# A graph-network layer on one core: row broadcasts in eight transfers, loads held back by the planner, three `g` banks and two `a` banks, 11 gather buffers

## The chip, the cores and the metric

One core of a Trainium2 chip runs the whole program. The time is device microseconds of one execution, from the first to the last work of the core; lower is better. The kernel before took 502.47 us (median of three runs, 501.62 to 507.94).

## The reference

Node features `x` (6,250 x 128, f32) and 100,000 edges, sorted by destination, each with a source, a destination and a type 0 or 1. For every edge a message is made from the source's row, with one of two weight matrices by type; messages are added up per destination; the node's own product is added; then relu, the residual and a layer norm:

```
Xs = X[src]
m_data = Xs @ W_data.T + b_data
m_ctrl = Xs @ W_control.T + b_control
msg = jnp.where((edge_types == 0)[:, None], m_data, m_ctrl)
agg = jax.ops.segment_sum(msg, dst, num_segments=X.shape[0])
out = relu(agg + (X @ W_self.T + b_self))
x   = layernorm(x + out)
```

## The kernel before

**The message table.** A message depends only on the source and the type, so the kernel makes all 2 x 6,250 of them once. 25 steps of two node blocks each (L467 to L501) load pieces of `xt` (the transposed features), multiply in f32 on TensorE (L483), and split each result into three bf16 parts, 3 x 128 = 384 columns: ACT writes the first part (L488), TensorE subtracts it (L491), ACT or VectorE writes the second (L494), VectorE the third (L495). `m3` holds the 98 tiles (49 node blocks x 2 types) of 128 rows in SBUF; a copy goes to DRAM as `table` (L499).

**Windows.** The first 27 x 160 destinations are done window by window, in groups of 1, 2, 4, 4, 4, 4, 4 and 4 windows (`GROUPS`). `ranks` (L611) prepares a group: it loads the edges of each window (`win`), makes one-hots of their source tiles (`hots`, L681), counts with matmuls into the bank `rk` (for the first group `ga`) which place each edge takes among the edges of its tile (L692, read by VectorE at L706), and scatters source row and destination of the edge to that place with matmuls into `vt` (L742; 21 for each window). The result is copied to `vs` (L755), stored to DRAM as `packed` (L762) and read back. Edges beyond 32 places of a tile go into a list of 64, whose messages are gathered from `table` by GpSimd (`sr`, L851) and moved to `gl` (L858).

`sums` (L884) then works through the windows. One transfer of 784 KB broadcasts the window's 32 x 98 row numbers to all 128 partitions (`rows`, L893); VectorE compares them with the partition number, in two halves (L901), which makes the one-hots of the sources; VectorE makes the one-hots of the destinations, `hot2` (L909). Then come 25 steps `g` of four tiles each. **Stage 1** (L922): four matmuls, one for each strip of 32 output partitions, pick 4 x 32 messages out of `m3` into a PSUM bank `g`. **The copy** (L425): ACT, rarely VectorE, turns the bank into bf16, `gs`. **Stage 2** (L936, L939): four matmuls of 384 and three of 128 columns add the 128 messages to the window's 160 destinations, in the PSUM bank `a`. After the last step VectorE adds up the three parts (L551) and ACT copies the rest (`bs`, L949); `close` (L514) does relu, residual, layer norm and the stores.

**Gathered destinations.** The other 1,930 destinations lie in 16 blocks of up to 125. GpSimd gathers 128 messages at a time from `table` (`t_msg`, L1016, 263 times, eight buffers), VectorE makes one-hots for six gathers at once (`t_hot`, L1010, two buffers), and TensorE adds them up in the bank `ga` (L1023). This runs beside the windows and fills in between their matmuls.

**Order.** Every instruction goes through `Plan` (L92). At build time it lays all of them on a time axis, with a duration, a due time and assumed latencies (`HOP`, `lat`) for each, takes on each engine the ready operation with the earliest due time, and writes the resulting order out. On the chip each engine keeps that order: what waits holds up all that stands behind it on its engine. SyncE (SP) starts nearly all transfers. Transfers started by SP and ACT use eight completion semaphores in turn, and a start waits until the transfer eight places before it has landed. PSUM has eight banks: four `g`, one `a`, and one each for `rk`, `ga` and `vt`. The product steps of the start use the `g` and `a` banks (L470).

Of the kernel before, what the change touches and what calls it, by code (L numbers as in the profile page):

```python
# [10 lines left out]
F32 = mybir.dt.float32  # L11
BF16 = mybir.dt.bfloat16
I32 = mybir.dt.int32
# [8 lines left out]
P = 128  # L22
# [60 lines left out]
class Op:  # L83
    __slots__ = ("alts", "due", "lat", "deps", "after", "left", "ready", "start", "end", "out",
                 "index", "engine")

    def __init__(self, alts, due, lat):
        self.alts, self.due, self.lat = alts, due, lat
        self.deps, self.after, self.out = [], [], []


class Plan:  # L92
    HOP = {"PE": 0.22, "ACT": 0.15, "DVE": 0.11, "POOL": 0.12, "SP": 0.12}
    OWN = {"DVE": 0.09, "ACT": 0.12}
    OTHER = 0.5

    def __init__(self):
        self.ops, self.rings = [], {}

    def add(self, engine, dur, fn, due, r=(), w=(), lat=0.0):  # L100
        alts = engine if isinstance(engine, list) else [(engine, dur, fn)]
        op = Op(alts, due, lat)
        op.index = len(self.ops)
        self.ops.append(op)
        deps = set()
        for items, writes in ((r, False), (w, True)):
            for item in items:
                b, key = item if isinstance(item, tuple) else (item, None)
                for k, (ws, rs) in b.keys.items():
                    if key is None or k is None or k == key:  # L110
                        deps.update(ws)
                        if writes:
# [12 lines left out]
        return op  # L125
# [4 lines left out]
    def run(self):  # L130
# [31 lines left out]
        while len(order) < n:  # L162
# [20 lines left out]
            for o in op.out:  # L183
                if op in o.deps:
                    same = op.lat == 0 and all(a == e for a, _, _ in o.alts)
                    lag = self.OWN.get(e, 0.0) if same else op.lat + self.HOP[e]
                    o.ready = max(o.ready, op.end + lag)
                    o.left -= 1
                if op in o.after:
                    o.ready = max(o.ready, op.start)  # L190
                    o.left -= 1
                if not o.left:
                    offer(o)
                    o.left = -1
# [47 lines left out]
def sums_over_windows(ctx, tc, x, xt, edges, w, bias, out, total):  # L242
# [16 lines left out]
    def C(shape, dtype, name):  # L259
        return Buf(plan, const, shape, dtype, name, 1)  # L260

    T0 = 36.0
    TW = 13.0
    LAT = 0.2
    G0, G1 = 0.0, -4
    GC = 1.3
    SPD = 0.45


# [4 lines left out]
    w_sb = C([D, D3], F32, "w_sb")  # L274
    b1 = C([1, D3], F32, "b1")
    add("ACT", 0.1, lambda: A.dma_start(w_sb.t, w), 0.0, [], [w_sb], lat=2.5)
    add("ACT", 0.1, lambda: A.dma_start(b1.t, bias), 0.0, [], [b1], lat=2.5)

# [83 lines left out]
    def count_rows():  # L362
# [8 lines left out]
    vec(0.5, 1, lambda: V.tensor_copy(row_i.t, row_f.t), [row_f], [row_i])  # L371
    er = C([NBD, RL, 3], I32, "er")
    add("POOL", 1.0, lambda: G.indirect_dma_start(
        out=er.t.rearrange("p k c -> p (k c)"), out_offset=None,
        in_=edges.rearrange("(p k) c -> p (k c)", k=RL),
        in_offset=bass.IndirectOffsetOnAxis(ap=row_i.t[:, 0:1], axis=0)),
        0.5, [row_i], [er], lat=3.5)
# [3 lines left out]
    vec(0.6, RL, lambda: V.tensor_copy(dst_f.t, er.t[:, :, 1]), [er], [dst_f])  # L381
    vec(0.6, RL, lambda: V.tensor_scalar(less.t, dst_f.t, bound_p.t, None, op0=ALU.is_lt,
# [15 lines left out]
    def load_edges(b, n, out_, due, buf, key, engine):  # L398
# [13 lines left out]

    left = C([1, D3], F32, "left")
# [3 lines left out]
    add("ACT", 0.4, lambda: A.copy(brows.t[:1], b1.t), 0.5, [b1], [brows])  # L417
    vec(0.5, D3, lambda: V.tensor_sub(left.t, b1.t, brows.t[:1]), [b1, brows], [left])
    add("ACT", 0.4, lambda: A.copy(mid.t, left.t), 0.5, [left], [mid])
    vec(0.5, D3, lambda: V.tensor_sub(brows.t[2 * R : 2 * R + 1], left.t, mid.t), [left, mid],  # L420
        [(brows, 2)])
# [19 lines left out]
    XB = [12, 12, 12, 13]  # L441
    XC = 4 * WN
    xts = []
# [167 lines left out]
    def ranks(gi, w0, nw, when, step, engines):  # L611
# [237 lines left out]
        for pr in range(nh):  # L849
# [34 lines left out]
    def sums(gi, w0, nw, placed):  # L884
# [5 lines left out]
        for i in range(nw):  # L890
            due = T0 + (w0 + i) * TW
            sp = B(work, [P, R, NT], BF16, "rows", 3, R * NT)
            add("SP", SPD, lambda i=i, sp=sp: S.dma_start(  # L893
                sp.t.rearrange("p r c -> p (r c)"),
                packed[gi, i // 2, (i % 2) * 64 : (i % 2) * 64 + R, :]
                .rearrange("r c -> (r c)")[None, :].to_broadcast([P, R * NT])),
                due - 12, [(packed_b, gi)], [sp], lat=3.0)
            half = R // 2
# [7 lines left out]
            for ci, (c0, c1) in enumerate(zip(cuts, cuts[1:])):  # L906
# [51 lines left out]
    def gathered(bis, when, step):  # L958
# [37 lines left out]
        for j, bi in enumerate(bis):  # L996
# [6 lines left out]
            for k in range(nt):  # L1003
                at = start + step * k
                kk = j * nt + k
                if k % KB == 0:
                    kn = min(KB, nt - k)
                    hot = B(work, [P, kn, P], BF16, "t_hot", 2, KB * P)
                    s4 = [P, kn, P // 2, 2]
                    vec(at + 1, kn * P, lambda hot=hot, kk=kk, kn=kn, s4=s4: V.tensor_tensor(  # L1010
                        hot.t.rearrange("p k (c d) -> p k c d", d=2),
                        iota1_b.t[:, :P].rearrange("p (c d) -> p c d", d=2)[:, None]
                        .to_broadcast(s4), code.t[:, kk : kk + kn, None, :].to_broadcast(s4),
                        op=ALU.is_equal), [code, (iota1_b, 0)], [hot], 0.52)
                m = B(work, [P, D3], BF16, "t_msg", 8)
                add("POOL", GC, lambda m=m, kk=kk: G.indirect_dma_start(  # L1016
# [199 lines left out]
```

## Time and profile before

| | |
|---|---|
| Median of three runs | 502.47 us |
| The profiled execution | 505.74 us, span 504.2 us, mean granted clock 0.959 |
| TensorE (PE) | 453.6 us busy, 90% of the span |
| VectorE (DVE) | 394.9 us, 78% |
| ScalarE (ACT) | 349.0 us, 69% |
| GpSimd (POOL) | 299.2 us, 59% |
| Transfers | 76.83 MB, mean 152 GB/s |

TensorE's first instruction stands at 7.4 us, the first window's work begins at 56.4 us, the last matmul of a window ends at about 492 us, and the rest is the last close. A busy TensorE need not be at its peak: matmuls overlap, and a short stall between two of them lies under the end of the first. So besides the share of busy time, the number of matmuls in a stretch is counted. In a stretch of 5 us from 60 us on, in which PE has no idle time and the clock is 1.00, there are mostly 140 to 160 of them. The clock is TensorE's granted clock as a share of full speed.

### The profile page before, as it was taken

Reading aid. Unit: us, or ns where it says so; the run is one execution under the profiler, and the core shown is the slowest. Engines: PE = TensorE matmul, PEld = TensorE weight load, DVE = VectorE, ACT = ScalarE, POOL = GpSimd, SP = SyncE. Lnnn points to the kernel's source line nnn. Section 1 sums busy time; section 2 is a strip of 40 time slices with the busy share of each in tenths; the row PEclk is TensorE's granted clock in tenths of the full one; section 3 lists DMA queues with packets and bytes.
Section 4 is the critical chain, followed back from the end, with each engine's and each line's share of the span. In section 5 each row is a group of like instructions: output and inputs, shape, how many; then the busy total and the mean of one; then the engine's idle time right before and its main releaser. Section 6 shows DMA issues by size and latency. Waiting matters only on the chain.

```text
span 504.2 us, 26935 instructions
## 1 busy us (share of the span) xinstructions
PE 453.6 (90%) x11461; PEld 364.8 (72%) x11461; DVE 394.9 (78%) x1271; ACT 349.0 (69%) x891; POOL 299.2 (59%) x290
## 2 busy tenths in 40 slices
PE   4999986996999998999699999999899999897990
PEld 2666654884778787787598877878678887686880
DVE  6599987998898988989598899888948787553343
ACT  2476763763767876778486788777867778595881
POOL 1000057775467687857676677777676757776720
PEclk9999996998799999999899999999989999898997
DMA  4399977346552466634655256662654426644320
GB/s 145 122 287 342 292 149 241 100 106 208 143 149 66 132 172 179 179 87 134 195 160 171 64 139 195 200 169 69 195 154 130 153 68 155 225 116 135 79 69 19
DMA packets 63117, 76.83 MB, mean 152 GB/s; under 512 B 21000, under 2 KB 52893, under 8 KB 62989
## 3 DMA queue, kind: packets, MB, share of 16 engines
q1 hardware_dynamic: 49147, 47.35, 29.8%
q0 software_dynamic: 13456, 27.42, 21.3%
q8 instruction: 91, 1.49, 1.2%
q10 hardware_dynamic: 386, 0.26, 0.2%
q14 instruction: 37, 0.30, 0.2%
HBM read 60.50 MB, written 13.17 MB: 146 GB/s over the span
## 4 chain that ended last, share of the span: by engine, by line
PE 67%; DMA 16%; DVE 7%; ACT 5%; issue 2%; SPq 1%; POOL 0%; ACTq 0%; DVEq 0%; POOLq 0%
PE g L922 20%; PE a L936 17%; PE rk L692 8%; DMA rows<-packed 7%; PE ga L1023 7%; DMA t_msg<-table,t_idx 6%; PE g L483 3%; PE a L939 3%; PE vt L742 3%; ACT gs L425 3%; DMA packed<-vs 2%; DVE rows L901 1%; ACT to_d L432 1%; PE ga L692 1%; PE a L508 1%
## 5 line engine op out<-in xcount | busy, mean ns | idle before, releaser
L1016 POOL DMA_INDIRECT t_msg<-table,t_idx x263 | 278.0, 1057 | 113.8 <-PE ga L1023 42.5
L425 ACT CAST gs<-g 128x384 bf16<-128x384 f32 x639 | 270.2, 487 | 103.3 <-PE g L922 81.3
L922 PE MATMUL g<-m,rows 128*32 128x384 bf16 x2646 | 261.2, 338 | 7.2 <-DVE rows L901 5.3
L936 PE MATMUL a<-gs,hot 128*32 128x384 bf16 x2592 | 259.9, 335 | 2.8 <-ACT gs L425 1.9
L922 PEld LDWEIGHTS <-rows 128*32 128x32 bf16 x2646 | 159.5, 135 | 22.2 <-DVE rows L901 6.4
L939 PE MATMUL a<-gs,hot 128*32 128x128 bf16 x1944 | 164.1, 222 | 0.0
L1023 PE MATMUL ga<-t_msg,t_hot 128*32 128x384 bf16 x1036 | 125.7, 332 | 16.7 <-DMA t_msg<-table,t_idx 10.7
L936 PEld LDWEIGHTS <-hot 128*32 128x32 bf16 x2700 | 121.9, 97 | 24.8 <-issue 7.9
L706 DVE TENSOR_REDUCE slot<-rk 128x4 f32<-128x392 f32 (+1 forms) x138 | 76.8, 556 | 23.9 <-PE rk L692 12.5
L939 PEld LDWEIGHTS <-hot 128*32 128x32 bf16 x2025 | 86.8, 99 | 10.7 <-issue 0.7
L692 PE MATMUL rk<-hots,tri 128*32 128x392 bf16 (+1 forms) x588 | 73.1, 327 | 0.7 <-issue 0.7
L692 PE MATMUL rk<-hots,rest 128*32 128x392 bf16 (+1 forms) x556 | 68.6, 328 | 2.6 <-DVE slot L706 2.6
L1023 PEld LDWEIGHTS <-t_hot 128*32 128x32 bf16 x1036 | 53.2, 98 | 23.7 <-issue 19.5
L909 DVE TENSOR_TENSOR hot<-iota_b,to_d 128x1280 bf16<-128x1280 bf16 (+1 forms) x81 | 67.6, 842 | 0.1
L851 POOL DMA_INDIRECT sr<-table,at x14 | 16.7, 1191 | 46.8 <-DMA xr<-in_x 38.6
L901 DVE TENSOR_SCALAR rows<-rows,pid 128x1568 bf16<-128x1568 bf16 x54 | 34.3, 638 | 12.8 <-DMA rows<-packed 12.7
L1010 DVE TENSOR_TENSOR t_hot<-iota_b,t_code 128x768 bf16<-128x768 bf16 (+2 forms) x47 | 24.7, 526 | 19.3 <-PE g L922 11.2
L681 DVE TENSOR_TENSOR hots<-iota_b,st 128x784 bf16<-128x784 bf16 (+1 forms) x83 | 38.6, 487 | 0.5 <-PE vt L742 0.4
L692 PEld LDWEIGHTS <-rest 128*32 128x32 bf16 x624 | 28.1, 98 | 10.6 <-issue 8.3
L692 PEld LDWEIGHTS <-tri 128*32 128x32 bf16 x672 | 30.1, 99 | 3.7 <-issue 1.4
L551 DVE TENSOR_REDUCE s<-a 128x128 f32<-128x384 f32 x27 | 15.0, 557 | 21.2 <-ACT bs L425 7.7
L425 ACT CAST m<-g 128x512 bf16<-128x512 f32 x20 | 11.6, 587 | 13.8 <-PE g L491 13.8
(188 smaller groups left out, 545.4 us busy)
## 6 DMA issues: line engine op xcount, KB each, us to landing
rows<-packed SPq DMA_DIRECT2D x27, 784.0 KB
table<-m SPq DMA_DIRECT2D x12, 768.0 KB
t_msg<-table,t_idx POOLq DMA_INDIRECT x263
rows<-in_xt SPq DMA_DIRECT2D x8, 256.0 KB
xc<-in_xt SPq DMA_DIRECT2D x6, 320.0 KB
gl<-sr SPq DMA_DIRECT2D x27, 48.0 KB
xr<-in_x SPq DMA_DIRECT2D x5, 256.0 KB
out<-xr SPq DMA_DIRECT2D x5, 256.0 KB
```

The costliest lines, as they stand in the source:

```text
L425: [("ACT", act(cols), lambda: A.copy(o(), src())), ("DVE", dve(cols), lambda: V.tensor_copy(o(), src()))], None, None, due, r, w, lat)
L681: lambda k=k, kn=kn, ci=ci, hs4=hs4: V.tensor_tensor(hv(ci)[:, k - ks[ci] : k - ks[ci] + kn].rearrange("p k w (c d) -> p (k w) c d", d=2), ...
L692: T.matmul(acc.t[R * j : R * j + R, c * wide : c * wide + wide], wt.t[:, R * j : R * j + R], one(k).rearrange("p w c -> p (w c)"), start=s ...
L706: vec(due, len(m) * wide, lambda r=r, m=m: V.tensor_reduce(slot.t[:, r:KT:L, :], acc.t[:, : len(m) * wide].rearrange("p (k w c) -> p k w c ...
L901: add("DVE", dve(half * NT, 0.335), lambda sp=sp, rs=rs: V.tensor_scalar(sp.t[:, rs], sp.t[:, rs], pid1.t, None, op0=ALU.is_equal), due - ...
L909: lambda i=i, hot2=hot2, s4=s4, c0=c0, c1=c1: V.tensor_tensor(hot2.t[:, c0:c1].rearrange("p g (c d) -> p g c d", d=2), iota1_b.t.rearrange ...
L922: T.matmul(gp.t[R * t : R * t + R, :D3], sp.t[:, :, 4 * g + t], m3.t[:, 4 * g + t, :], start=True, stop=True)
L936: T.matmul(a.t[R * j : R * j + R, :D3], hot2.t[:, g, R * j : R * j + R], gs.t, start=g == 0, stop=False, skip_group_check=True)
L939: T.matmul(a.t[R * c : R * c + R, D3:], hot2.t[:, g, P:], gs.t[:, c * D : (c + 1) * D], start=False, stop=last, skip_group_check=True)
L1010: vec(at + 1, kn * P, lambda hot=hot, kk=kk, kn=kn, s4=s4: V.tensor_tensor(hot.t.rearrange("p k (c d) -> p k c d", d=2), iota1_b.t[:, :P]. ...
L1016: add("POOL", GC, lambda m=m, kk=kk: G.indirect_dma_start(out=m.t, out_offset=None, in_=table[:, :], in_offset=bass.IndirectOffsetOnAxis(a ...
L1023: T.matmul(ga.t[R * i : R * i + R, :D3], hot.t[:, k % KB, R * i : R * i + R], m.t, start=k == 0, stop=False, skip_group_check=True)
```

## The change

There are eight edits, nearly all of them in data that the planner reads.

- The row broadcast of a window becomes eight transfers of 16 partitions (`RP`), due 14 us before the window and 0.9 us apart (`RA`, `RS`); it was one, due 12 us before.
- The planner keeps an operation back by a `slack` after its inputs are ready: 6 us for transfers of `t_raw`, `win`, `xc`, `t_xc`, `xr`, `xrg`, `xb` and the outputs, 3 us for `gl`, 2 us for the store of `packed`, where the transfer is due after 60 us on SP; 3 us for the gather `sr`.
- `g` has three banks instead of four and `a` two instead of one; the product steps are divided accordingly.
- The planner's allowance behind the copies out of `g` and behind the count's reduction (`LAT`) is halved.
- Group 0 is due at 0 instead of 3, and group 1 at 8 instead of 18.
- `t_msg` has 11 buffers instead of eight.
- `t_hot` has three buffers instead of two.
- To make room, `er`, `b1` and `left` of the start use the buffers `xc` and `two`.

The number of matmuls of each kind is the same in both kernels.

```diff
+    SLACK = dict.fromkeys(("t_raw", "win", "xc", "t_xc", "xr", "xrg", "xb", "out"), 6.0)
+    SLACK.update(gl=3.0, packed_b=2.0)
+    FROM = 60.0
...
+        kind = [(i[0] if isinstance(i, tuple) else i).name for i in w] or ["out"]
+        if engine == "SP" and due > self.FROM:
+            op.slack = self.SLACK.get(kind[0], 0.0)
...
-                    o.ready = max(o.ready, op.end + lag)
+                    o.ready = max(o.ready, op.end + lag + o.slack)
...
-    LAT = 0.2
+    LAT = 0.1
...
+    RP, RA, RS = 8, 14, 0.9
...
-    b1 = C([1, D3], F32, "b1")
+    early = lambda: B(work, [P, 48 * R], BF16, "two", 2, 48 * R)
+    b1_, left_ = early(), early()
...
-    er = C([NBD, RL, 3], I32, "er")
+    er_ = B(work, [P, XC], F32, "xc", 2, XC)
...
-        mp = B(ps, [P, 512], F32, *(("a", 1) if q % 5 > 3 else ("g", 4)))
+        mp = B(ps, [P, 512], F32, *(("a", 2) if q % 5 > 2 else ("g", 3)))
...
-                d3 + 1, [(at, pr), table_b], [sr], lat=2.0)
+                d3 + 1, [(at, pr), table_b], [sr], lat=2.0).slack = 3.0
...
-            add("SP", SPD, lambda i=i, sp=sp: S.dma_start(
-                sp.t.rearrange("p r c -> p (r c)"),
-                packed[gi, i // 2, (i % 2) * 64 : (i % 2) * 64 + R, :]
-                .rearrange("r c -> (r c)")[None, :].to_broadcast([P, R * NT])),
-                due - 12, [(packed_b, gi)], [sp], lat=3.0)
+            for j in range(RP):
+                add("SP", SPD, lambda i=i, sp=sp, j=j: S.dma_start(
+                    sp.t[P // RP * j : P // RP * (j + 1)].rearrange("p r c -> p (r c)"),
+                    packed[gi, i // 2, (i % 2) * 64 : (i % 2) * 64 + R, :]
+                    .rearrange("r c -> (r c)")[None, :].to_broadcast([P // RP, R * NT])),
+                    due - RA + RS * j, [(packed_b, gi)], [(sp, ("p", j))], lat=2.0)
...
-            a = B(ps, [P, 512], F32, "a", 1)
+            a = B(ps, [P, 512], F32, "a", 2)
...
-                gp = B(ps, [P, 512], F32, "g", 4)
+                gp = B(ps, [P, 512], F32, "g", 3)
...
-                    hot = B(work, [P, kn, P], BF16, "t_hot", 2, KB * P)
+                    hot = B(work, [P, kn, P], BF16, "t_hot", 3, KB * P)
...
-                m = B(work, [P, D3], BF16, "t_msg", 8)
+                m = B(work, [P, D3], BF16, "t_msg", 11)
...
-            when, step, engines = 3.0, 0.9, ["SP"]
+            when, step, engines = 0.0, 0.9, ["SP"]
...
-            when, step, engines = 18.0, 1.1, ["SP", "ACT"]
+            when, step, engines = 8.0, 1.1, ["SP", "ACT"]
```

More of the change, by code (lines that the diff above doesn't have):

```diff
@@ L84 @@
     __slots__ = ("alts", "due", "lat", "deps", "after", "left", "ready", "start", "end", "out",
-                 "index", "engine")
+                 "index", "engine", "slack")
     def __init__(self, alts, due, lat):
-        self.alts, self.due, self.lat = alts, due, lat
+        self.alts, self.due, self.lat, self.slack = alts, due, lat, 0.0
         self.deps, self.after, self.out = [], [], []
@@ L260, in C @@
         return Buf(plan, const, shape, dtype, name, 1)
+    XC = 4 * WN
     T0 = 36.0
     TW = 13.0
-    LAT = 0.2
+    LAT = 0.1
     G0, G1 = 0.0, -4
@@ L274, in sums_over_windows @@
     w_sb = C([D, D3], F32, "w_sb")
-    b1 = C([1, D3], F32, "b1")
+    early = lambda: B(work, [P, 48 * R], BF16, "two", 2, 48 * R)
+    b1_, left_ = early(), early()
+    b1 = lambda: b1_.t.bitcast(F32)[:1, :D3]
+    left = lambda: left_.t.bitcast(F32)[:1, :D3]
     add("ACT", 0.1, lambda: A.dma_start(w_sb.t, w), 0.0, [], [w_sb], lat=2.5)
-    add("ACT", 0.1, lambda: A.dma_start(b1.t, bias), 0.0, [], [b1], lat=2.5)
+    add("ACT", 0.1, lambda: A.dma_start(b1(), bias), 0.0, [], [b1_], lat=2.5)
     iota_f = C([P, P], F32, "iota_f")
@@ L371, in sums_over_windows @@
     vec(0.5, 1, lambda: V.tensor_copy(row_i.t, row_f.t), [row_f], [row_i])
-    er = C([NBD, RL, 3], I32, "er")
+    er_ = B(work, [P, XC], F32, "xc", 2, XC)
+    er = lambda: er_.t.bitcast(I32)[:NBD, : RL * 3].rearrange("p (k c) -> p k c", c=3)
     add("POOL", 1.0, lambda: G.indirect_dma_start(
-        out=er.t.rearrange("p k c -> p (k c)"), out_offset=None,
+        out=er_.t.bitcast(I32)[:NBD, : RL * 3], out_offset=None,
         in_=edges.rearrange("(p k) c -> p (k c)", k=RL),
         in_offset=bass.IndirectOffsetOnAxis(ap=row_i.t[:, 0:1], axis=0)),
-        0.5, [row_i], [er], lat=3.5)
+        0.5, [row_i], [er_], lat=3.5)
     dst_f = C([NBD, RL], F32, "dst_f")
@@ L380, in sums_over_windows @@
     in_row = C([NBD, 1], F32, "in_row")
-    vec(0.6, RL, lambda: V.tensor_copy(dst_f.t, er.t[:, :, 1]), [er], [dst_f])
+    vec(0.6, RL, lambda: V.tensor_copy(dst_f.t, er()[:, :, 1]), [er_], [dst_f])
     vec(0.6, RL, lambda: V.tensor_scalar(less.t, dst_f.t, bound_p.t, None, op0=ALU.is_lt,
@@ L410, in load_edges @@
         add(engine, dur, fn, due, [first] if b else [], [(buf, key)], lat=2.0)
-    left = C([1, D3], F32, "left")
     mid = C([1, D3], BF16, "mid")
@@ L416, in sums_over_windows @@
     vec(0.2, D3, lambda: V.memset(brows.t, 0.0), [], [brows], 0.3)
[L417 to L420, printed above, removed]
+    add("ACT", 0.4, lambda: A.copy(brows.t[:1], b1()), 0.5, [b1_], [brows])
+    vec(0.5, D3, lambda: V.tensor_sub(left(), b1(), brows.t[:1]), [b1_, brows], [left_])
+    add("ACT", 0.4, lambda: A.copy(mid.t, left()), 0.5, [left_], [mid])
+    vec(0.5, D3, lambda: V.tensor_sub(brows.t[2 * R : 2 * R + 1], left(), mid.t), [left_, mid],
         [(brows, 2)])
@@ L441, in sums_over_windows @@
     XB = [12, 12, 12, 13]
-    XC = 4 * WN
     xts = []
```

## The prediction

> **What bounds the kernel now.** I read the page's busy shares and the rows of the clock first, then stretches of 5 us from 60 us on, then the chain that ended last, then the waits.
>
> ```profile
> PE 453.6 (90%) x11461; PEld 364.8 (72%) x11461; DVE 394.9 (78%) x1271; ACT 349.0 (69%) x891; POOL 299.2 (59%) x290
> PE   4999986996999998999699999999899999897990
> ...
> PEclk9999996998799999999899999999989999898997
> ```
>
> TensorE (PE) has most of the span; its dips, and the dips of its clock below them, are what can be won. Stretches of 5 us show a dip's depth (columns: stretch, length, busy time of PE, weight load, DVE, ACT and POOL, each with its number of instructions, granted clock, DMA share, GB/s):
>
> ```profile
> 70.00:75.00 5.00, 2.83 (x49) 1.58 (x49) 3.21 (x13) 1.60 (x5) 3.40 (x4) 0.85 0.81 178
> 75.00:80.00 5.00, 2.43 (x39) 0.92 (x31) 3.56 (x10) 0.26 (x1) 3.78 (x5) 0.81 0.90 310
> 80.00:85.00 5.00, 3.75 (x52) 2.32 (x55) 4.13 (x10) 2.27 (x6) 3.78 (x5) 0.53 0.87 222
> ...
> 120.00:125.00 5.00, 3.28 (x51) 1.76 (x51) 3.06 (x11) 0.00 (x0) 3.76 (x4) 0.62 0.94 354
> 125.00:130.00 5.00, 3.25 (x47) 2.03 (x51) 4.67 (x11) 1.92 (x5) 4.08 (x4) 0.50 0.86 264
> ...
> 160.00:165.00 5.00, 5.00 (x144) 4.10 (x139) 4.96 (x10) 4.25 (x11) 4.08 (x4) 1.00 0.26 69
> ...
> 240.00:245.00 5.00, 1.26 (x26) 1.06 (x29) 1.75 (x4) 0.61 (x3) 3.99 (x4) 0.91 0.84 252
> ...
> 455.00:460.00 5.00, 2.34 (x71) 1.88 (x67) 1.82 (x4) 2.61 (x7) 3.71 (x4) 0.92 0.64 221
> ```
>
> A full stretch holds some 150 matmuls, 30 a microsecond (144 at 160 us). So a stretch with n of them has lost (150 - n)/30 us, a slow clock included: 70 to 90 us (49, 39, 52, 120 matmuls) 11.3 us, 115 to 135 us (105, 51, 47, 130) 8.9 us. The chain names the causes (columns: start, length, what):
>
> ```profile
> 69.59 4.30 DMA packed<-vs
> 73.91 5.89 DMA rows<-packed
> ...
> 116.47 2.15 DMA packed<-vs
> 118.64 6.13 DMA rows<-packed
> ...
> 234.80 8.90 DMA t_msg<-table,t_idx
> ```
>
> The first two dips are the trip through DRAM: group 1's last scatter ends at 68.2 us, group 2's at 116.1 us, and the window behind it cannot start before store, broadcast and comparison are done, 13 and 10 us later. The others are late gathers (around 190, 240 and 365 us: 98, 26 and 121, 113 and 71 matmuls, 10.7 us lost) and a row broadcast that SP started late, at 453.19 us, behind loads of `x` (455 to 465 us: 71 and 116 matmuls, 3.8 us). The waits (total, times, longest) give the gathers' side:
>
> ```profile
> POOL t_msg L1016 <- PE ga L1023: 42.5, 63, 5.4
> ...
> PE ga L1023 <- DMA t_msg<-table,t_idx: 10.7, 7, 4.2
> ...
> PE a L936 <- ACT gs L425: 1.9, 3, 1.2
> ```
>
> GpSimd waits 42.5 us for a free buffer and then runs from 224 to 239 us without a pause, one gather each 1.25 us (0.95 us and a 0.30 us gap), trying to catch up. The last line says that PE hardly waits for the copy out of `g`. That is the cover which this change takes away.
>
> **Earlier ranks** (`when` 3 to 0 and 18 to 8). In the instruction order of the built kernels, group 1's last scatter stands behind 88 of window 0's 98 stage-1 matmuls before, behind 32 after. Window 0 takes about 11 us for its 98, so the scatter comes 56/98 x 11 = 6.3 us earlier and the first dip shrinks by as much, and by part of the slow slice behind it (clock 0.53): 7 us of 11.3. Group 2's stands behind all 294 stage-1 matmuls of the first three windows before, behind 268 after: 26/98 x 14 us (window 2's length) = 3.7 us, with the clock 4 of 8.9. The 48 count matmuls that now come before window 0 are moved, not added. If only that happens, and window 0 starts later for it, this is worth nothing; I keep 0 to 14 and take **-11**.
>
> **11 gather buffers, three for one-hots, and `sr` 3 us later.** Three more buffers are 3 x 1.25 = 3.75 us more lead for POOL, where it waited for one before; the longest wait of PE for a gather is 4.2 us. VectorE's 3.3 us wait for a `t_hot` buffer at 241 us goes as well. Of the 10.7 us lost I take **-8**, between 0 (if the lead is already used up by the catching up) and -11.
>
> **Slack in SP's order.** In the new order the last windows' row pieces stand ahead of the `x` loads that held them up at 451 to 453 us. What waits for longest in SP's queue now is behind them. Of 3.8 us I take **-3** (0 to -4). `out` before them still waits for a close; that close belongs to a window before, so it is done by then.
>
> **A second `a` bank.** At the other 24 window ends the time from stage 2 to the next window's stage 2 exceeds the matmuls between by about 0.3 us: 0 to -7 us. The matmuls put there fill it already; I take **-1**.
>
> **Eight row transfers.** SP starts 427 transfers instead of 238, at some 0.4 us each (the middle row start took 383 ns): 180 us of 504, so SP has room. A broadcast took 5 to 6 us from start to landing where a window waited for it. Eight pieces: seven starts of 0.42 us and one small landing, for which the shortest `packed` store stands (2.15 us): 5.1 us. So each piece costs nothing while eight are in flight; if a start has to wait for the piece eight places before, the window gets 2 us later. Seven group starts: -6 to +14, I take **+1**. VectorE's comparison waits for eight semaphores instead of one, 27 times, at 17 to 50 ns each: under 5 us on an engine with 22% idle, 0.
>
> [...] The trace shows 5 to 6 us for the whole, beside other traffic, and no run here shows a piece.
>
> **Three `g` banks and half the allowance.** This is the price. The trace's records give, from stage 1's matmuls to the first of stage 2 of the same step, 0.97 us at the shortest: 0.33 us matmul, 0.10 to ACT, 0.48 copy, 0.06 back. In the 44% of the steps where stage 2 starts right behind the copy, the mean is 1.19 us, because the copy first waited for ACT. In the new order I counted the PE work that stands between the two, each group of four strips at 160 ns (their pitch in the trace). Before: 1.39 us in the middle, 9 of 675 steps below 1.0 us. After: 1.07 us, 85 below 1.0, 341 below 1.07, 419 below 1.2. If the chain takes 0.99, 1.07, 1.12 or 1.20 us, what is missing adds up to 8, 22, 40 or 71 us after and 1, 2, 4 or 9 before; two steps are in flight at a time, so one stall serves two and PE loses half: +4, +10, +18 or +31. The mean of 1.19 comes from groups of stage 1 in a row (0.16 us apart in a quarter of the steps before, 0.37 after, and ACT takes a copy each 0.4 us), so the queue at ACT gets shorter and I stay nearer to the shortest: 1.07 us, **+10**.
>
> **Start buffers.** `er`, `b1` and `left` in used buffers make one `xc` load wait; the window needs it 40 us later. 0.
>
> **Sum.** -11 - 8 - 3 - 1 + 1 + 10 = -12 us. The profiled execution took 505.7 us, 3.3 above the median; 505.7 - 12 = 493.7, and against the median of 502.5 **490 us**, 2.4% less. A change under 2%, 10 us, can't be told from none.
>
> **Rivals.**
> - *The copy takes it all back.* With 1.12 to 1.17 us in the chain, PE loses 18 to 27 us instead of 10, and the gains of 22 are gone: 498 to 507 us, within 2%. For it: ACT is at 69% and copies come in order. Against it: the larger distance between stage-1 groups.
> - *The dips only move.* Window 0 starts later by what is moved ahead of it, and gathers stay late because POOL is at its pace (277 x 1.25 = 346 of the 415 us in which it gathers): without the 11 and half of the 8, 505 us. Also within 2%.
> - *The copy becomes the bound* (slower). One mechanism: three banks let PE run no more than three steps ahead, and each wait of ACT for its other work (normalisations of 0.45 us each, casts of 0.26 us) now stalls PE. It decides from a chain of 1.22 us on, where the loss passes the gains by 10 us; at 1.20 to 1.25 PE loses 31 to 38 us: 511 to 518 us. For it: the measured mean of 1.19.
> - *The copy costs nothing.* With +4 and the full gains (-14, -11, -4, -3) 474 to 480 us.
>
> **Chances.** Forecast (480 to 493) 0.42, copy costs nothing 0.10, first rival 0.23, dips only move 0.09, copy the bound 0.16. So faster by over 2% 0.50 (the upper end of the forecast case falls short of it), within 2% 0.33, slower 0.17. The range leaves out the fastest and the slowest ends: 475 to 512; the forecast's own is 480 to 493.
>
> **What the new profile would show.** Earlier ranks: over 100 matmuls in each stretch between 72 and 88 us, and no clock under 0.8 there. Gathers: PE's wait for `t_msg` under 3 us in all, POOL's wait for `ga` shorter. Slack: no row start behind `x` loads in the last group. Pieces: some 0.4 us between row starts, the eighth landing 5 to 6 us behind the first start. The copy: PE's wait for `gs` above 1.9 us, and full stretches with 140 rather than 150 matmuls. The forecast is wrong if full stretches fall below 140 (slower), or the dips stay at 70 and 120 us.

## The result, and the profile after

The changed kernel took **540.09 us** (median of four runs, 534.1 to 542.47), the kernel before beside it 503.63 (501.62 to 507.94): 1.067 times the time, 95% interval 1.054 to 1.080. This ratio, like those below, leaves out runs in a slower state; the medians do not. The forecast was 490, in a range of 475 to 512. The change is slower, by more than the slowest rival.

The page of the changed kernel, profiled at 538.46 us: busy times, PE and its clock in 40 slices, the share of the 16 DMA engines that was busy in the same slices, and `q1`, the queue of the transfers that SP and ACT start (packets, MB, share of 16 engines). Behind it the last two rows of the kernel before.

```profile
PE 460.6 (86%) x11461; PEld 370.6 (69%) x11461; DVE 395.0 (74%) x1273; ACT 354.8 (66%) x889; POOL 299.6 (56%) x290
...
PE   5999966997789989898798999679979799769991
...
PEclk9999989998989999999799999798999989999997
DMA  4699797359782796629946288471597715975410
...
q1 hardware_dynamic: 52171, 47.36, 39.0%
```

```profile
DMA  4399977346552466634655256662654426644320
...
q1 hardware_dynamic: 49147, 47.35, 29.8%
```

No engine has much more to do (PE is busy 7 us longer with the same matmuls, ACT 6), and q1 moves the same 47 MB, but its packets now keep the 16 engines busy for 39.0% of a longer span, where it was 29.8%. The DMA row has nine slices of 90% or more, seven of them behind the start of the first window; the kernel before had three, none wholly behind it.

Stretches of 5 us of the changed kernel (columns as before):

```profile
75.00:80.00 5.00, 3.18 (x50) 1.88 (x49) 4.68 (x10) 1.46 (x4) 4.08 (x4) 0.66 1.05 158
...
85.00:90.00 5.00, 2.20 (x57) 1.87 (x60) 1.90 (x7) 1.47 (x5) 3.78 (x5) 1.00 0.66 183
120.00:125.00 5.00, 2.98 (x66) 1.72 (x59) 4.38 (x12) 0.74 (x3) 3.94 (x4) 1.00 1.06 176
...
240.00:245.00 5.00, 4.88 (x142) 3.84 (x132) 4.92 (x21) 3.63 (x13) 4.08 (x4) 1.00 0.67 128
255.00:260.00 5.00, 3.15 (x75) 2.41 (x75) 1.02 (x7) 2.56 (x6) 3.77 (x4) 1.00 1.01 203
260.00:265.00 5.00, 3.10 (x51) 2.43 (x54) 3.65 (x7) 0.98 (x3) 2.84 (x3) 0.53 0.87 194
335.00:340.00 5.00, 1.25 (x37) 0.77 (x29) 1.27 (x3) 0.47 (x1) 3.78 (x5) 0.88 1.00 220
```

The two first dips are still there. The late gathers at 240 us are gone (26 matmuls before, 142 now). New dips stand at 255 to 265 and at 335 us, and there VectorE is idle too (1.02 of 5 us busy from 255 us, 1.27 from 335), while the DMA share is 1.01 and 1.00: the waits below say that VectorE waits for a transfer, and PE for VectorE. Full stretches still hold 140 to 150.

The chain of the changed kernel (start, length, what) names the transfer, and the waits (total, times, longest) name the places; behind them two waits of the kernel before:

```profile
126.30 7.06 DMA rows<-packed
...
245.48 7.15 DMA rows<-packed
252.65 7.29 DMA rows<-packed
...
473.13 6.07 DMA rows<-packed
```

```profile
POOL t_msg L1027 <- PE ga L1034: 76.1, 73, 7.3
...
DVE rows L912 <- DMA rows<-packed: 38.0, 14, 4.8
PE rk L702 <- DVE slot L716: 32.6, 16, 4.5
...
DVE rows L912 <- DMA gl<-sr: 12.1, 4, 4.1
...
PE a L947 <- ACT gs L436: 3.9, 9, 1.2
...
PE ga L1034 <- DMA t_msg<-table,t_idx: 1.9, 1, 1.9
```

```profile
DVE rows L901 <- DMA rows<-packed: 12.7, 9, 3.4
...
PE rk L692 <- DVE slot L706: 2.6, 5, 1.0
```

VectorE's row comparison (L901 before, L912 now) waited 12.7 us for its rows before. Now VectorE is idle ahead of it for 68.1 us in all, 38.0 of them put down to the rows and nearly all the rest to other transfers (12.1 to `gl`); it stands idle before 25 of the 27 comparisons. Behind the comparison on VectorE stands the reduction of the count (`slot`), for which PE waits 32.6 us instead of 2.6. From 60 us to the last matmul of a window PE is idle for 57.6 us in all, 31.9 of them ahead of the count. PE's wait for a gather fell from 10.7 to 1.9 us, as forecast; the wait for the copy rose only from 1.9 to 3.9.

The trace's record of each packet shows the transfer itself. A row packet (6,272 bytes, one partition) took 239 ns in the middle before and takes 520 now; all of them together 956 and 1,733 us of engine time. From the first to the last packet of a window's broadcast it was 3.6 us in the middle (2.9 to 4.7 for the inner 80%) and is 7.8 (6.5 to 9.7).

### The profile page after: what moved, and what is told of

It reads as the page before. It is cut to its first block, busy times and chain, and to the rows that moved or that the text cites. A ratio compares the mean times of both kernels' runs of the same rounds, so it can differ in the third digit from the quotient of the medians.

```text
span 536.9 us, 27273 instructions
## 1 busy us (share of the span) xinstructions
PE 460.6 (86%) x11461; PEld 370.6 (69%) x11461; DVE 395.0 (74%) x1273; ACT 354.8 (66%) x889; POOL 299.6 (56%) x290
## 4 chain that ended last, share of the span: by engine, by line
PE 57%; DMA 20%; ACT 6%; DVE 6%; SPq 6%; issue 3%; POOL 1%; ACTq 0%; DVEq 0%
PE g L933 16%; PE a L947 15%; DMA rows<-packed 11%; PE rk L702 6%; PE ga L1034 6%; SPq L904 4%; ACT gs L436 3%; PE a L950 3%; PE vt L752 2%; ACT to_d L443 2%; DVE rows L912 2%; DMA gl<-sr 2%; DMA xr<-in_x 2%; PE g L493 2%; DMA t_msg<-table,t_idx 1%
## 5 line engine op out<-in xcount | busy, mean ns | idle before, releaser
L436 ACT CAST gs<-g 128x384 bf16<-128x384 f32 x640 | 275.0, 482 | 110.7 <-PE g L933 91.8
L933 PEld LDWEIGHTS <-rows 128*32 128x32 bf16 x2646 | 166.4, 135 | 21.0 <-issue 6.8
L947 PEld LDWEIGHTS <-hot 128*32 128x32 bf16 x2700 | 119.7, 97 | 37.7 <-issue 21.3
L1034 PE MATMUL ga<-t_msg,t_hot 128*32 128x384 bf16 x1036 | 104.8, 334 | 2.3 <-DMA t_msg<-table,t_idx 1.9
L950 PEld LDWEIGHTS <-hot 128*32 128x32 bf16 x2025 | 84.7, 98 | 8.2 <-issue 2.2
L702 PE MATMUL rk<-hots,rest 128*32 128x392 bf16 (+1 forms) x556 | 57.6, 331 | 33.5 <-DVE slot L716 32.6
L912 DVE TENSOR_SCALAR rows<-rows,pid 128x1568 bf16<-128x1568 bf16 x54 | 34.8, 657 | 68.1 <-DMA rows<-packed 38.0
L702 PE MATMUL rk<-hots,tri 128*32 128x392 bf16 (+1 forms) x588 | 62.6, 328 | 1.4 <-issue 1.4
L702 PEld LDWEIGHTS <-rest 128*32 128x32 bf16 x624 | 25.7, 97 | 44.9 <-issue 42.5
L1034 PEld LDWEIGHTS <-t_hot 128*32 128x32 bf16 x1036 | 49.6, 99 | 8.5 <-issue 4.1
L752 PEld LDWEIGHTS <-two 128*64 128x64 bf16 x567 | 14.7, 111 | 7.4 <-DVE two L743 2.4
```

The lines of the kernel that those rows point to most:

```text
L436: [("ACT", act(cols), lambda: A.copy(o(), src())), ("DVE", dve(cols), lambda: V.tensor_copy(o(), src()))], None, None, due, r, w, lat)
L702: T.matmul(acc.t[R * j : R * j + R, c * wide : c * wide + wide], wt.t[:, R * j : R * j + R], one(k).rearrange("p w c -> p (w c)"), start=s ...
L752: T.matmul(vv()[q : q + 64, i // 2, :], two.t[:, (k - k0) * nw + i].rearrange("p f r -> p (f r)"), one(k)[:, i, :], start=k == 0 and i < 2 ...
L912: add("DVE", dve(half * NT, 0.335), lambda sp=sp, rs=rs: V.tensor_scalar(sp.t[:, rs], sp.t[:, rs], pid1.t, None, op0=ALU.is_equal), due - ...
L933: T.matmul(gp.t[R * t : R * t + R, :D3], sp.t[:, :, 4 * g + t], m3.t[:, 4 * g + t, :], start=True, stop=True)
L947: T.matmul(a.t[R * j : R * j + R, :D3], hot2.t[:, g, R * j : R * j + R], gs.t, start=g == 0, stop=False, skip_group_check=True)
```

## The experiments

Ratios are to the kernel before, run beside on the same chip. Four versions ran on a chip where the kernel before takes 498 us, much as in the result (503.6); the others on three chips on which the same program takes 650 to 663 us, for a reason that was not found; the last section has what was seen of it. They are kept apart.

### On a chip like that of the result

All four ran side by side, with the kernel before at 498.21 us (493.11 to 506.13).

**The changed kernel once more.**

> The changed kernel unchanged, beside the other three of this call. About 1.04 times the kernel before where that takes 650 us or more (1.067 where it takes 503); VectorE idle ahead of the row comparison 15 to 25 us in all (68 us where the kernel before takes 503), TensorE's wait of the count for VectorE's reduction 7 to 8 us (33 us).

536.83 us, 1.073 (1.063 to 1.083): the loss is there again.

**The broadcast whole, all else as changed.**

```diff
-    RP, RA, RS = 8, 14, 0.9
+    RP, RA, RS = 1, 14, 0.9
```

> The changed kernel with the broadcast whole. Theory In-order (what costs is the comparison that stands on VectorE for a slow broadcast, with the count's reductions behind it): idle ahead of the comparison under 4 us, the count's wait 2 to 3 us, and the time 0.5 to 1.5% below the changed kernel on this call's chip (4 to 7% where the kernel before takes 503 us). Theory Late rows (PE itself waits for rows that are late): the same time, but PE's own wait for the comparison is what shrinks. Theory Copy: within 0.3% of the changed kernel.

**486.34 us, 0.979 (0.974 to 0.985).** One of the eight edits costs 50.5 us, and the other seven together win 11.9 (the whole transfer still stands 14 us before its window and not 12). This version is faster than both kernels, than the one before by 2.1% (1.5 to 2.6). Its page (profiled at 483.58 us) and its waits:

```profile
PE 444.5 (92%) x11461; PEld 363.7 (75%) x11461; DVE 394.9 (82%) x1273; ACT 352.7 (73%) x889; POOL 297.5 (62%) x290
...
PE   4999978998999899899998999999989999999990
...
PEclk9999998999999999999999999999999999999995
DMA  4589976428553655724647254663555625645220
...
q1 hardware_dynamic: 49147, 47.35, 31.4%
```

```profile
POOL t_msg L1027 <- PE ga L1034: 31.8, 61, 4.6
...
DVE rows L912 <- DMA rows<-packed: 5.2, 4, 2.8
...
PE a L947 <- ACT gs L436: 4.7, 12, 0.7
...
PE ga L1034 <- DMA t_msg<-table,t_idx: 3.4, 5, 1.2
...
PE rk L702 <- DVE slot L716: 3.1, 3, 2.4
```

VectorE's wait for rows and PE's wait for the count are nearly gone. PE is idle for 18.2 us from 60 us to the last matmul of a window, and of the 39.4 us less than in the changed kernel 28.8 are the wait for the count (31.9 and 3.1). The DMA row has no full slice behind the start. The row of the clock is at 9 nearly throughout. Theory Copy falls: the three banks are still in this kernel.

**The eight transfers kept, the comparison put later.**

```diff
-                    due - RA + RS * j, [(packed_b, gi)], [(sp, ("p", j))], lat=2.0)
+                    due - RA + RS * j, [(packed_b, gi)], [(sp, ("p", j))], lat=10.0)
```

> The changed kernel with all eight transfers, but the planner told that a piece takes 10 us to land instead of 2, so that it puts the comparison behind other work of VectorE. The transfers stay as slow. Theory In-order: idle ahead of the comparison under 6 us, the count's wait 2 to 4 us, and at least half of what the whole broadcast wins, 0.3 to 1.2% below the changed kernel (3 to 6% where the kernel before takes 503 us). Theory Late rows: no better than the changed kernel, or worse, since the comparison comes later still.

527.44 us, 1.061 (1.054 to 1.068): 9.4 us better than the changed kernel, 1.8%, and 41 us worse than with the whole broadcast. The two ratios are only 0.012 apart, 6 us, and their intervals overlap; but five of the six runs of the changed kernel are slower than all six of these. That speaks against theory Late rows, and it is less than half of what theory In-order claimed. The waits, and the chain:

```profile
POOL t_msg L1027 <- PE ga L1034: 60.7, 73, 7.9
...
PE ga L1034 <- DMA t_msg<-table,t_idx: 12.9, 15, 3.0
...
PE rk L702 <- DVE slot L716: 6.7, 8, 1.6
...
DVE rows L912 <- DMA rows<-packed: 0.6, 3, 0.2
```

```profile
256.76 6.72 DMA t_msg<-table,t_idx
...
333.19 6.52 DMA t_msg<-table,t_idx
...
444.11 7.53 DMA t_msg<-table,t_idx
```

VectorE no longer waits, and PE's wait for the count went from 32.6 to 6.7 us (29.1 in the changed kernel beside it). But two other costs have come. The gathers are late: PE waits 12.9 us for them instead of 1.9 (4.0 in the changed kernel beside it). A gather that is in flight together with a row broadcast takes about 4 us in the middle from issue to the last packet, the others 2.5; that is so whether the broadcast is whole or split, but 162 of 276 gathers met one in the changed kernel and 100 with the whole broadcast. It does not tell why they are later here than in the changed kernel, since here 152 met one. And the first windows of the groups start later, since the planner now puts them behind a landing that it takes to be 10 us away: at the seven group starts, the time between the last stage 2 of one window and the first of the next, beyond the matmuls between them at 30 a microsecond, sums to 29.4 us, where it was 5.0 in the changed kernel and 1.7 with the whole broadcast.

**The broadcast whole, the comparison put earlier.**

```diff
-    RP, RA, RS = 8, 14, 0.9
+    RP, RA, RS = 1, 14, 0.9
...
-                    sp.t[:, rs], sp.t[:, rs], pid1.t, None, op0=ALU.is_equal), due - 4 + q,
+                    sp.t[:, rs], sp.t[:, rs], pid1.t, None, op0=ALU.is_equal), due - 10 + q,
```

> The changed kernel with the broadcast whole, but the comparison due 10 us before its window instead of 4, so that VectorE comes to it before the rows have landed although the transfer is quick. Theory In-order: idle ahead of the comparison up to 10 to 30 us again, and the time 0.3 to 1.5% above the kernel with the whole broadcast. Theory Late rows: the same as the kernel with the whole broadcast, since the rows are ready no later.

488.89 us, 0.984 (0.978 to 0.990): 2.5 us above the whole broadcast, 0.5%; the two intervals overlap, but five of its six runs are slower than all six of the whole broadcast. Its waits:

```profile
DVE rows L912 <- DMA rows<-packed: 20.4, 16, 3.0
...
PE rk L702 <- DVE slot L716: 6.1, 8, 1.5
```

20 us of idle VectorE (5.2 with the whole broadcast) go with 3 us more of waiting for the count. So waits of at most 3 us were mostly covered here; those of the changed kernel go up to 4.8 and are three times as many microseconds.

### On three chips that run the kernel before in 650 to 663 us

**Each part of the split, first round** (the kernel before at 662.88 us): the broadcast whole; eight pieces of every eighth partition; the split alone in the kernel before; two pieces of 64 partitions.

```diff
-                    sp.t[P // RP * j : P // RP * (j + 1)].rearrange("p r c -> p (r c)"),
+                    sp.t[j : P : RP].rearrange("p r c -> p (r c)"),
```

The diff is that of the strided pieces; the others change `RP` to 1 or 2, or add only the new transfers to the kernel before.

> The changed kernel with the row broadcast as one transfer again (all else of the change stays; due time 14 us before the window). Narrow theory (a transfer to 16 neighbouring partitions moves its 6,272-byte packets at half the speed: 520 ns in the middle against 239): packets back at 240 ns, a broadcast's packets within 3 to 4 us instead of 6 to 10, the 36 us are gone and what is left of the gains shows: 485 to 505 us. Starts theory (eight starts and landings on SP cost the time, whatever the packets do): the same, 485 to 505. Copy theory (three g banks and the halved allowance make PE wait for ACT): stays at 525 or more, with packets at 240 ns.

> The changed kernel with the same eight transfers of 16 partitions, but each takes every eighth partition instead of 16 neighbours; the order of all instructions is the same. Narrow theory: packets back near 240 ns, a broadcast in 4 to 5 us, 485 to 510 us. Starts theory: packets may be faster, but the time stays at 530 to 545 us. Copy theory: 530 to 545 us.

> The kernel before with only the row broadcast cut into eight transfers of 16 neighbouring partitions (due 14 us before the window, 0.9 us apart). Narrow and starts theory: 525 to 545 us, packets at 500 ns in the middle (narrow) or at 240 ns (starts). Copy theory: 500 to 510 us.

> The changed kernel with two transfers of 64 neighbouring partitions for a broadcast. Narrow theory: 64 partitions are half as narrow a target as the whole and four times as wide as 16; packets between 240 and 350 ns, time between the whole and the eight, nearer to the whole: 490 to 515 us. Starts theory: 2 starts instead of 8, 490 to 510 us. Copy theory: 525 or more.

| | ratio | row packet, ns | first to last packet of a broadcast, us |
|---|---|---|---|
| whole | 1.029 (1.022 to 1.036) | 246 | 3.4 |
| every eighth partition | 1.049 (1.041 to 1.057) | 291 | 6.2 |
| split alone | 1.013 (1.004 to 1.022) | 585 | 7.6 |
| two pieces of 64 | 1.028 (1.018 to 1.037) | 444 | 4.8 |

The packets answer theory Narrow's question: pieces of neighbouring partitions have slow packets, 64 neighbours as well as 16, and eight pieces of strided partitions do not, so it is not the number of pieces. The times answer nothing of the sort: the strided pieces, with quick packets, are the slowest, and the whole broadcast is no faster than two pieces. The strided pieces change a second thing, too: starting one takes SP 587 ns in the middle, where a piece of 16 neighbours takes 418. On such a chip a window takes some 20 us instead of 14, and in the changed kernel VectorE waits 10.8 us for its rows there, not 38.0.

**Second round** (before at 662.76 us): three of these again, and the whole broadcast with four `g` banks, one `a` bank and the old allowance (`LAT`).

> The changed kernel with the row broadcast whole again (one transfer of 128 partitions, still due 14 us before the window); all other edits stay. Theory Narrow (pieces of 16 neighbouring partitions run at half the packet speed): row packets back to about 240 ns, a broadcast from first to last packet 3 to 4.5 us, the wait of the row comparison for its rows down from 38 to about 13 us, time 505 to 515 us. Theory Starts (eight starts and landings cost, whatever the packets do): the same 505 to 515. Theory Copy (three g banks cost the 36 us): 530 to 540, with the broadcast as quick but the time hardly moved.

> The changed kernel with eight row transfers still, but each writes every eighth partition instead of 16 neighbouring ones; the starts, their order and their bytes are the same. Theory Narrow: packets near 240 to 290 ns, time 510 to 525 us, most of the way back to the kernel with the whole broadcast. Theory Starts: packets quick and the time still 530 to 542. Theory Copy: 530 to 540.

> The kernel before with the split of the row broadcast alone (eight transfers of 16 partitions, due 14 us before, 0.9 us apart); four g banks, eight gather buffers and the old planning stay. Theory Narrow and theory Starts: packets 520 to 590 ns, a broadcast 6 to 9 us, ratio to the kernel before 1.04 to 1.07. Theory Copy: 0.995 to 1.015.

> The changed kernel with the row broadcast whole and with four g banks, one a bank and the old allowance: what is left of the change is the earlier ranks, the slack and the gather buffers. By the prediction's terms for these (-11, -8, -3) 482 to 490 us, ratio 0.96 to 0.975; if the dips only move, 500 to 506. Against the kernel with three g banks and a whole broadcast it is to be 10 us quicker if the copy costs what the prediction said, none if the copy costs nothing, over 25 us by theory Copy.

1.026 (1.018 to 1.034), 1.048 (1.040 to 1.057), 1.011 (1.002 to 1.020): as in the first round. With four banks 1.020 (1.012 to 1.027); the intervals with three and with four overlap, but all four runs with four banks (676.2 to 678.2 us) are faster than all four with three (680.3 to 682.3), by 0.7%.

**Third round** (before at 651.09 us): the changed kernel itself, and with the split kept and the four banks back.

> The changed kernel unchanged, once more, to have it on the chip on which the other runs were made. Where the kernel before takes about 503 us, it is to be 534 to 542, ratio 1.055 to 1.08. Where the kernel before takes about 663 us: the parts there were, as ratios, 1.011 for the split alone and 1.026 for all but the split. If the parts add, 1.035 to 1.045 (686 to 693 us); if eight pieces of 16 neighbouring partitions hurt more beside three g banks than alone, above the 1.048 of eight pieces of every eighth partition.

> The changed kernel, split included, with four g banks, one a bank and the old allowance. Theory Narrow: the rows stay late (wait of the row comparison 30 us or more), and the time is within 10 to 15 us of the changed kernel. Theory Copy: 25 us or more below it.

1.039 (1.035 to 1.043) and 1.041 (1.036 to 1.046): no difference beside the split, against theory Copy.

**Fourth round** (before at 650.52 us): the whole broadcast, and the whole broadcast with four banks and no slack (all values of `SLACK` and that of `sr` zero).

> The changed kernel with the row broadcast whole again, once more, for a chip on which the kernel before takes about 503 us. There, theory Narrow and theory Starts: 505 to 515 us; theory Copy: 530 to 540. On a chip where the kernel before takes 650 us or more: 1.02 to 1.03 times the kernel before, as the two runs of it there.

> The changed kernel with the broadcast whole, four g banks, one a bank, the old allowance, and no slack: what is left of the change is the earlier ranks, 11 gather buffers, three one-hot buffers. If the slack is what costs (loads and gl held back until they are late), 0.98 to 1.00 of the kernel before; if it costs nothing, the 1.02 of the kernel with the slack on a chip where the kernel before takes 650 us or more, and 482 to 490 us where it takes 503.

1.038 (1.030 to 1.045) and 1.023 (1.016 to 1.031). On this chip the banks, the allowance and the slack together cost 1.4%; which of them is not separated.

**Last round** (before at 661.9 us): the strided pieces and the whole broadcast with four banks once more.

> The changed kernel with eight row transfers, each to every eighth partition instead of 16 neighbouring ones. Where the kernel before takes about 500 us, with the whole broadcast at 0.979 and eight pieces of 16 neighbours at 1.073 of it: theory Busy engines (the slow packets of neighbours keep all 16 DMA engines busy, and rows, gathers and loads land late): packets 240 to 300 ns, idle ahead of the row comparison 10 to 30 us, 0.99 to 1.03. Theory Starts (eight starts and a broadcast of 5 to 8 us cost, whatever the packets do): 1.05 to 1.08. Where the kernel before takes 650 us or more, 1.048 as before.

> The changed kernel with the broadcast whole, four g banks, one a bank and the old allowance; earlier ranks, slack and gather buffers stay. The same with three g banks took 0.979 of the kernel before where that takes about 500 us. If the three banks cost the 10 us of the prediction: 0.955 to 0.965 (476 to 482 us). If the copy costs nothing: 0.975 to 0.985. Where the kernel before takes 650 us or more, 1.02 as before.

1.055 (1.051 to 1.059) and 1.026 (1.022 to 1.029), as on these chips before. What strided pieces would do where the kernel before takes 500 us stays open.

## Why the prediction was wrong

**Eight row transfers: +1 us, measured +50.** This is the step that failed, in two places.

*The piece was taken to be as quick as the whole, only smaller.* "Eight pieces: seven starts of 0.42 us and one small landing" made 5.1 us. From the first start to the last packet it is 10.1 us in the middle, where the whole broadcast takes 4.9 (from first to last packet 7.8 and 3.5). Half of the 10.1 is the starts: the eighth stands 5.0 us behind the first and not 2.9, since SP waits for other transfers between them (for the piece eight places before, among others: 17.0 us in 31 waits in all, none over 1.0). The other half is the eighth piece, some 5 us where 2.15 were put in, and its packets are slow: one to a partition of a group of 16 takes 520 ns and not 239.

Measured from first to last packet, a broadcast took 3.5 us whole, 4.8 in two pieces of 64, 6.2 in strided pieces (whose eighth start stands 5.1 us behind the first) and 7.8 in pieces of 16 (the second and third on the chips of 650 to 663 us, where the first and last are 3.4 and 7.5). Why the packets of neighbouring partitions are slow is not shown. Nor does their time alone give this order: 5.0 of the 7.8 us lie between the first and the eighth start, and strided pieces, with packets of 291 ns, take longer than two pieces of 64, with 444.

*It was charged at seven group starts only.* I had the rows come late for a window; they hardly do. In the changed kernel the second half of the comparison starts 0.7 to 29 us before the window's first matmul, over 9 us before it in all but the seven group starts, and PE's own wait for it is 1.3 us in all (5.3 before). The cost lies elsewhere. VectorE keeps its order, and the planner, which takes a piece to land after 2 us, puts the comparison close behind the last piece; so VectorE stands still ahead of it in 25 of 27 windows, 68.1 us in all, and the count's reduction behind it makes PE wait 32.6 us. My sentence on VectorE counted eight semaphores at 17 to 50 ns and "22% idle, 0" (216 waits at 50 ns would be 10.8 us, not under 5), and left out what is queued behind the waiting instruction. In the changed kernel this wait is the largest part that the traces show: 28.8 of the 39.4 us that PE is idle longer than with the whole broadcast. Moving the comparison away (-9.4 us) takes it out, and that 41 us remain shows that this alone does not help: the gathers are then late, and a planner that allows for a slow transfer starts the groups later. How the 41 us divide between these two, and how much of the slowness is the eight starts and how much the slow packets, is not settled.

*Part of it was lost at half clock.* Counting as the prediction did (30 matmuls a microsecond is full), the changed kernel lost 108.0 us from 60 us to the last matmul of a window, the one with the whole broadcast 52.8; the difference of 55.2 is that of the spans, 55.0 us. Of it, 17.4 were lost while the clock stood at half: 34.1 us of half clock in the changed kernel, 3.4 with the whole broadcast. The kernel before has 34.1 us of it too, so against that kernel the clock explains none of the loss.

**The rest of the sum: -13 forecast, -11.9 measured** (486.34 against 498.21). That the two agree so closely is partly luck, as the terms and the remarks below them show. Term by term, from the profile of the version with the whole broadcast:

- *Earlier ranks, -11.* About right. The stretches, to be held against the 49, 39, 52 and 120 and the 105, 51, 47 and 130 matmuls of before:

```profile
70.00:75.00 5.00, 3.10 (x57) 2.60 (x60) 4.34 (x8) 1.80 (x4) 4.00 (x4) 0.78 0.92 298
75.00:80.00 5.00, 4.21 (x90) 2.57 (x83) 3.87 (x10) 1.47 (x5) 2.15 (x3) 0.87 0.77 224
80.00:85.00 5.00, 4.58 (x129) 3.55 (x123) 5.00 (x11) 2.62 (x7) 3.15 (x3) 1.00 0.26 61
...
115.00:120.00 5.00, 4.63 (x114) 3.40 (x111) 5.00 (x14) 2.73 (x9) 4.08 (x4) 1.00 0.97 335
120.00:125.00 5.00, 5.00 (x149) 4.18 (x142) 4.86 (x19) 4.55 (x13) 4.09 (x4) 1.00 0.68 202
```

  With 124 from 85 us on, the first dip has lost 6.7 us instead of 11.3; with 149 and 144 from 125 us on, the second 1.5 instead of 8.9: 12.0 together, divided otherwise than I had it (7 and 4). A part of the first dip only moved: from 60 to 70 us there are now 105 and 123 matmuls, where there were 163 and 140. Held against the time at which the kernel before had issued as many matmuls, the version with the whole broadcast is 1.6 us ahead at 60 us and 10.2 at 135, a gain of 8.6.
- *Gathers, -8.* Right: PE's wait for them 10.7 to 3.4 us.
- *Slack, -3.* The dip at 455 us, with 71 matmuls before, is gone: no stretch between 375 and 465 us holds fewer than 130 now. The slack was not tried alone where the kernel before takes 500 us.
- *Three `g` banks, +10, and the second `a` bank, -1.* Together too dear. Losses of at most 1 us from the stage 2 of one step to that of the next, again at 30 matmuls a microsecond, sum to 35.9 us before and 36.4 with these banks and a whole broadcast, where +9 was forecast. Inside the windows they rose by 8.3 us (27.4 to 35.7), and at the 19 window ends that are no group start they fell by 6.6 (6.9 to 0.3). That would fit a copy that costs nearly its 10 us and an `a` bank that wins 7 and not 1; but the order changed as well, and neither was tried alone where the kernel before takes 500 us, so only the sum is shown. PE's wait for `gs` is 1.9 and 4.7 us. From the start of the last stage-1 matmul to stage 2 the middle is 1.05 us now, 1.36 before: the new order took more out of the queue at ACT than it took out of PE's cover. (In the changed kernel the same losses are 45.7 us. I read that as the copy first; it is the disturbance by the rows, since it is gone with them.)

Two remarks on this sum. The spans of the two profiles differ by 22.3 us (504.2 and 481.9), not by 12, because the profiled execution of before was a long one: 505.7 us against a median of 498.2 on the chip of the second. And 18 of the 22 lie in half-clock time (20.2 us lost in it before, 1.8 with the whole broadcast), which a few short dips more or less decide.

**The rivals.** None was right. The slower one named the copy and its 1.22 us chain; the way from stage 1 to stage 2 became shorter. "The dips only move" came nearest in kind: what was won at 240 us was lost at 260 and 335, but through a transfer that I had counted as harmless. Of the signs that the prediction named, the dips at 70 and 120 us did stay, and the eighth piece landed 10 and not 5 to 6 us behind the first start.

## What to carry to other kernels

Before a transfer is cut by partitions, measure one of its pieces: here the packets of a piece of 16 neighbouring partitions took 520 ns instead of 239, the same 47 MB kept the DMA engines busy for 39.0% of the span instead of 31.4%, and eight starts and slow packets together turned 3.5 us into 7.8. A transfer that gets slower need not be paid where its data are used; here it was paid where an engine that keeps its order waits for it (VectorE was idle for 68.1 us ahead of the comparison, and PE for 32.6 us ahead of the count behind it): look at what stands behind the waiting instruction, in every repetition and not only where the data are urgent. And when eight edits come together, undo the one whose row the profile lacks first: here the other seven together were worth keeping on the chip of the result's kind.

## What was not expected of the hardware

**Half clock came in spells of 3.41 us, behind stretches with few matmuls.** All half-clock spells up to the last window last 3.4 us or a multiple: the trace's records of the clock have 3.413, 6.827 and 10.240 us before, 3.413 and 6.827 in the changed kernel. Laying windows of 3.413 us over six traces of chips like that of the result (from 58 us on), every window at full clock with 10.5 or fewer matmuls a microsecond was followed by half clock (29 windows; in the kernel before 6 of them, with 3.5 to 10.3, in the changed kernel 8, with 2.6 to 10.0), and of those with 10.8 or more only one, of 17.3. A full stretch has 30. So, as an estimate from these figures, a stall of a little over 2 us within a window costs some 1.7 us more behind it (half of 3.41). With the whole broadcast, where PE is idle for 18.2 us and not 57.6, the mean clock is 0.986 against 0.962.

**Three chips run the same program a third slower.** On one of them ACT's instructions of the changed kernel take 404 us in sum as on the other chip (405), VectorE's 483 and 484, and up to the first window the matmuls keep within 0.2 us of those of the other chip. But an idle ACT starts its copy later behind stage 1: where ACT had been idle for over 0.25 us, the time from the nearest end of a stage-1 matmul to the copy was 105 ns in the middle and at most 112 in 95 of 100 (134 copies); on the slow chip it was 271 ns in the middle and over 778 in a quarter (223 copies). What goes beyond 110 ns sums to 0.3 us on the one and to 116 on the other. From the copy to TensorE it was about 50 ns at the shortest on both. TensorE's weight loads (PEld) show idle time that nothing in the profile ends ("issue"), and ACT waits that the profile can put down to no instruction ("remote"); in the changed kernel there:

```profile
PEld L947 <- issue: 118.1, 181, 3.4
ACT gs L436 <- PE g L933: 93.3, 129, 2.7
...
ACT gs L436 <- remote: 49.8, 17, 10.0
```

The first line is 21.3 us on the other chip. Whether TensorE's matmuls end late there or their end is told late, and why, was not found. It changes which edit pays: the seven edits that win 2.1% where the kernel before takes 498 us lose 2.6 to 3.8% there, so the version with the whole broadcast is the better one only on chips like the first.
